# A two-layer attention and expert kernel: no background turn in the 16-key unit, two more pairs summed by VectorE at chunk ends, and a rearranged end

## The chip, the cores and the metric

The kernel runs on one core of a Trainium2 chip (trn2). The metric is the device time of one execution, in microseconds, as the median of several runs. A difference of 0.2% (12 us) is about what can be told from no change here.

## The reference, cut to what matters

```python
# x: (8, 128, 36, 36); 8 images, 128 channels, 1296 positions each
x = x + layer0(group_norm(x))      # 3x3 convolutions to q, k, v; softmax attention
                                   # (1296 queries, 34*34 keys); 1x1 convolutions, tanh
t = tokens(x)                      # (8, 1296, 128)

# layer 1, attention: additive scores
q, k = ln(t) @ Wq.T + bq, ln(t) @ Wk.T + bk
s = einsum('bijd,d->bij', tanh(q[:, :, None] + k[:, None]), w) + bw
t = t + einsum('bij,bjd->bid', softmax(s), ln(t))

# layer 1, experts: each of 64 experts chooses 8 tokens of each image
y = ln(t)
probs = softmax(y @ gate_w.T + gate_b, axis=tokens)      # per image and expert
topv, topi = top_k(probs over tokens, 8)
pooled = sum over the 8 of topv * y[topi]                # (64, 8 images, 128)
h = gelu(pooled @ weight1 + bias1); o = h @ weight2 + bias2
out = t + scatter_add(o * topv at topi)
```

## The kernel before

**The scores.** The sum over 128 channels of w·tanh(q+k) is written as 24 fractions, 16 over groups of 5 channels and 8 over groups of 6. For each fraction the numerator and the denominator are products of exponential features of the keys (`kf`) and of the queries (`qf`) over 32 or 64 rows. A **unit** is one tile of keys against one **chunk** of 432 queries: 8 images x 3 chunks x 11 key tiles. Ten key tiles have 128 keys and take 12 **slots** `k` = 0 to 11, each a pair of fractions; the eleventh has the 16 keys that remain and takes 2 slots. This **16-key unit** stands sixth in the list `order`, so a chunk has positions 0 to 4 (full units), 5 (the 16-key unit) and 6 to 10 (full units). Position 10 is the chunk's end. In all there are 2928 slots.

**A slot.** TensorE makes the denominators of the slot three ahead (`d`, L1086 and L1091, PSUM pool `ps_d` of 2 buffers) and the numerators of this slot (`n`, the same lines, one bank each of the 4-bank pool `ps_n`). ScalarE takes the logarithm (`lq`, L1109) and exp(-log) (L1112). VectorE multiplies numerator and reciprocal. For slots in `DVE_PAIRS` = (1, 4, 7, 10) VectorE multiplies in place in PSUM (L1137) and also adds the products to `accd` (L1139). For the others it writes the products to `rp` (L1143), and GpSimd adds these to `accp` (L1150, L1152). At a unit's end GpSimd folds `accp` and `accd` together (L1159, L1161), except in the very last unit, where VectorE does that; ScalarE takes the exponential of the score (`e`, L1172) seven slots later.

**The background.** The rest of the work is written as generators that yield between steps, in four lanes: `first_of_all` (the eight query feature blocks `pq` of the next chunk; scores of the 16-key unit), `urgent` (`attend`, the weighted sum of values, and keys), `gates` (expert gating of the image before), and `background` (layer 0 and the tokens and keys of the next image). A lane step that needs TensorE runs only in a **turn**, `matmul_turn` after slots 2, 5, 8 and 11, and after slot 1 of the 16-key unit. In the slot after the 16-key unit there is a turn for `first_of_all` alone. Each slot adds `PACE` ns to a balance, each step subtracts what `behind` says it costs, and no lane but `first_of_all` gets a step while the balance is below zero. PSUM tiles of lane steps (`aux`) come from the same 4 banks as the numerators. An engine carries out its instructions in the order written, so what stands behind a waiting instruction waits too.

Of the steps, one matters below. In layer 0's attention GpSimd adds up the exponentials of a chunk's 10 key tiles (`total`, L476, tile `tot`); a matmul with ones sums `tot` over partitions (`pt`), ScalarE inverts it (`ri`, L499 and L500).

**The end.** After the last slot the pools of the scores are closed, and ten weight tiles of 1 MB (`wts`) take their place in SBUF. Both are stacked from the same side. SyncE's queue then holds, in this order: ten weight loads (`load_next`, L1343 and L1345); the last chunk of `t2d`; the gates of images 0 to 6 from DRAM (21 loads, L1361); residual 4 (L1366); the store of image 7's gates (L987); residuals 5 to 7 (L1383); image 7's gates; the other 21 weight loads, each when a buffer comes free; the output. Meanwhile image 7's last chunk goes through `attend`, `gate_logits` and `gate_tokens` (softmax over tokens, `max` for the eight largest, `match_replace` to take them out, the difference, transposes, `ppool`), and then 16 groups of 4 experts run (`inner`, `turned`, `outer`).

Of the kernel before, what the change touches and what calls it, by code (L numbers as in the profile page):

```python
# [10 lines left out]
AF = mybir.ActivationFunctionType  # L11
# [44 lines left out]
LAG = 3  # L56
SHIFT = 6.5
DVE_PAIRS = (1, 4, 7, 10)
TURNS = (2, 5, 8, 11)
NEXT_AT = {k: IN_TURN[i : i + 2] for k, i in zip(TURNS, (1, 3, 5, 7))}  # L60
PACE = 400

# [9 lines left out]
def kernel(  # L72
# [56 lines left out]
    with ExitStack() as loop, ExitStack() as score:  # L129
# [9 lines left out]
        one = pool("one", 1, ctx)  # L139
        chunks = pool("chunks", 8)  # L140
        two = pool("two", 2)
        kfp = pool("kfp", 3, score, "right")
        kstp = pool("kstp", 3, score, "right")
        qfp = pool("qfp", NF + 1, score, "right")
        lp = pool("lp", 2, score, "right")
        rpp = pool("rpp", 3, score, "right")
        acc = pool("acc", 2, score, "right")
        ps_d = pool("ps_d", 2, score, "right", bass.MemoryType.PSUM)

        ps_n = pool("ps_n", 4, space=bass.MemoryType.PSUM)  # L150
# [120 lines left out]
        def matmuls(rest=0):  # L271
            return (True, rest)
# [338 lines left out]
        def tokens(b):  # L611
# [8 lines left out]
            for g in range(0, NKT, 4):  # L620
                tp = aux("tpl")
                some = list(range(g, min(g + 4, NKT)))
                for t in some:
                    o, n = KT[t]
                    turned_to(
                        tp[:n, (t - g) * C : (t - g + 1) * C], r[:, o : o + n], ident
                    )
                yield TAKE
                full = sum(KT[t][1] == 128 for t in some)
                nc.vector.tensor_copy(  # L630
                    tok[:, g : g + full, :],
                    tp[:, : full * C].rearrange("p (t c) -> p t c", c=C),
                )
# [38 lines left out]
            for g in range(0, NKT, 4):  # L672
                tp = aux("tpc")
                some = list(range(g, min(g + 4, NKT)))
                for t in some:
                    o, n = KT[t]
                    turned_to(
                        tp[:, (t - g) * 128 : (t - g) * 128 + n], xh[:n, t, :C], ident[:n, :n]
                    )
                yield TAKE  # L680
                lo, hi = KT[g][0], KT[some[-1]][0] + KT[some[-1]][1]
                nc.vector.tensor_copy(xT[:, lo:hi], tp[:, : hi - lo])
                yield matmuls()
# [204 lines left out]
        def gate_logits(b, chunks):  # L888
# [2 lines left out]
            t2, mv = attended[b]  # L891
            if b not in logits:
                logits[b] = (
                    big_tile("probs")[:E, :N],
                    small.tile([E, NCH], F32, tag="mx", name="mx"),
                )
            pr, mx = logits[b]
# [6 lines left out]
            def turned(c, name):  # L904
# [2 lines left out]
                    turned_to(tp[:, j * T : (j + 1) * T], t2[:T, c * TPC + j, :], ident[:T, :T])  # L907
                return tp, chunk_tile(name)

            for c in chunks:  # L910
                tp, tt = turned(c, "t2T")
                yield TAKE
                nc.vector.tensor_copy(tt, tp[:, :CH])
                nc.sync.dma_start(t2d[b][:, c * CH : (c + 1) * CH], tt)
                yield matmuls(1)
                for j0 in range(0, TPC, 2):
                    tp = aux("tp3")
                    for j in (j0, j0 + 1):
                        turned_to(tp[:T, j * C : (j + 1) * C], tt[:, j * T : (j + 1) * T], ident)
                    yield TAKE  # L920
                    behind[0] += 500
                    for j in (j0, j0 + 1):
                        t = c * TPC + j
                        nc.vector.tensor_scalar(
                            t2[:T, t, :], tp[:T, j * C : (j + 1) * C],
                            mv[:, t, 0:1], rs[:, t - tiles[0] : t - tiles[0] + 1],
                            ALU.subtract, ALU.mult,
                        )
                    yield matmuls()
            for c in chunks:  # L930
# [8 lines left out]
                    pr[:, c * CH : (c + 1) * CH], pg[:E, :CH], gb_s, None, ALU.add, ALU.max,  # L939
                    accum_out=mx[:, c : c + 1],  # L940
                )
                yield matmuls()

        def gate_tokens(b):


            t2, _ = attended.pop(b)
            pr, mx = logits.pop(b)
# [5 lines left out]
            inv = small.tile([E, 1], F32, tag="ginv", name="ginv")  # L954
            tot = small.tile([E, NCH], F32, tag="tot", name="tot")
            gt = big_tile("gt")[:E, :N]
            if b == NB - 1:
                nc.scalar.activation(pr, pr, AF.Exp, bias=nm, accum_out=tot[:, 0:1])
                nc.vector.reciprocal(inv, tot[:, 0:1])
                nc.scalar.activation(pr, pr, AF.Copy, scale=inv)  # L960
                nc.vector.max(out=top, in_=pr)
                nc.vector.match_replace(out=gt, in_to_replace=top, in_values=pr, imm_value=0.0)
                nc.vector.tensor_sub(gt, pr, gt)
            else:
                parts = [slice(c * CH, (c + 1) * CH) for c in range(NCH)]
                tops = gt[:, : NCH * 8].rearrange("p (c k) -> p c k", k=8)
# [17 lines left out]
                for cols in parts:  # L984
                    yield step()
                    nc.gpsimd.tensor_sub(gt[:, cols], pr[:, cols], gt[:, cols])
            nc.sync.dma_start(gd[b], gt)  # L987
            yield matmuls(3)
            half = NT // 2
            gT = []  # L990
            for g in range(2):
                tp = aux("tpg")
                for j in range(half):
                    t = g * half + j
                    turned_to(
                        tp[:T, j * E : (j + 1) * E], gt[:, t * T : (t + 1) * T], ident[:E, :E]
                    )
                yield TAKE
                gT.append(chunk_tile("gT")[:T, : half * E].rearrange("p (t e) -> p t e", e=E))
                nc.vector.tensor_copy(  # L1000
                    gT[g], tp[:T, : half * E].rearrange("p (t e) -> p t e", e=E)
                )
                yield matmuls(g)
            pp = aux("ppool")
            for t in range(NT):
# [270 lines left out]
        for p, (u, k) in enumerate(slots):  # L1276
# [61 lines left out]
        def load_next():  # L1338
# [199 lines left out]
```

## Time and profile before

| | before |
|---|---|
| median of 3 runs (lowest to highest) | 6026.3 us (6025.81 to 6030.31) |
| the profiled execution, and its span | 6030.93 us, 6028.9 us |
| TensorE busy / VectorE / ScalarE / GpSimd | 94% / 79% / 89% / 76% |
| mean granted TensorE clock | 0.991 |
| first and last logarithm (L1109) | 135.7 and 5883.6 us |
| last three weight loads asked for, from | 5987.9 us |

The span runs from the first to the last instruction of the profiled execution. Nearly all of it is the slot loop, from 136 to 5884 us. About 136 us precede it, and about 145 us follow. Busy shares are means over stages that have different limits, so the loop is read by units: the logarithm of each slot (L1109) occurs once per slot, and its start times cut the trace into units. "Unit (b, c, p)" below is image b, chunk c, position p, from the logarithm of its slot 3 to that of the next unit's slot 3.

### The profile page before, as it was taken

Reading aid. Unit: us, or ns where it says so; the run is one execution under the profiler, and the core shown is the slowest. Engines: PE = TensorE matmul, PEld = TensorE weight load, DVE = VectorE, ACT = ScalarE, POOL = GpSimd, SP = SyncE. Lnnn points to the kernel's source line nnn. Section 1 sums busy time; section 2 is a strip of 40 time slices with the busy share of each in tenths; the row PEclk is TensorE's granted clock in tenths of the full one; section 3 lists DMA queues with packets and bytes.
Section 4 is the critical chain, followed back from the end, with each engine's and each line's share of the span. In section 5 each row is a group of like instructions: output and inputs, shape, how many; then the busy total and the mean of one; then the engine's idle time right before and its main releaser. Section 6 shows DMA issues by size and latency. Waiting matters only on the chain.

```text
span 6028.9 us, 94410 instructions
## 1 busy us (share of the span) xinstructions
PE 5641.8 (94%) x33489; PEld 2944.7 (49%) x33489; DVE 4783.2 (79%) x9560; ACT 5358.1 (89%) x5993; POOL 4581.8 (76%) x2870
## 2 busy tenths in 40 slices
PE   8999999999999999999999999999999999988887
PEld 5554455545554454544545445554445544544433
DVE  4887878878887788877888777887878878788883
ACT  2999998999989999889998999999998998999991
POOL 5777877877778868878787777777877777787871
PEclk9999999999999999999999999999999999999997
DMA  1200021001110011100111001110011001110008
GB/s 60 70 23 23 29 72 40 24 22 45 58 42 21 23 61 42 42 23 22 65 38 39 23 25 61 42 36 23 25 63 52 21 25 34 66 50 26 28 21 291
DMA packets 150457, 270.43 MB, mean 45 GB/s; under 512 B 45600, under 2 KB 75680, under 8 KB 149984
## 3 DMA queue, kind: packets, MB, share of 16 engines
q1 hardware_dynamic: 149984, 264.39, 13.3%
q8 instruction: 264, 4.33, 0.3%
q14 instruction: 209, 1.71, 0.1%
HBM read 200.15 MB, written 63.93 MB: 44 GB/s over the span
## 4 chain that ended last, share of the span: by engine, by line
PE 58%; DVE 23%; ACT 8%; issue 7%; POOL 2%; DMA 1%; DVEq 0%; POOLq 0%; ACTq 0%
PE d L1086 19%; PE n L1086 12%; DVE rp L1143 9%; PE pa L278 7%; DVE n L1137 7%; ACT lq L1109 6%; PE pc L278 5%; DVE accd L1139 4%; PE s L278 3%; PE pk L278 3%; PE pq L278 2%; PE n L1091 1%; POOL accp L1152 1%; PE d L1091 1%; DMA w<-in_weight_dram 1%
## 5 line engine op out<-in xcount | busy, mean ns | idle before, releaser
L1152 POOL TENSOR_TENSOR accp<-accp,rp 128x864 f32<-128x864 f32 x1439 | 2911.1, 2023 | 965.9 <-DVE rp L1143 937.9
L1086 PE MATMUL n<-qf,kf 32*128 32x432 f32 (+1 forms) x11520 | 2996.1, 552 | 12.5 <-ACT qf L805 7.4
L1086 PE MATMUL d<-qf,kf 32*128 32x432 f32 (+1 forms) x11520 | 2777.8, 558 | 206.0 <-ACT lq L1109 196.8
L1109 ACT ACTIVATE lq<-d 128x864 f32<-128x864 f32 x2928 | 2480.2, 876 | 341.5 <-PE n L1086 254.3
L1143 DVE TENSOR_TENSOR rp<-n,lq 128x432 f32<-128x432 f32 x3912 | 2182.0, 600 | 701.6 <-PE n L1086 570.6
L1112 ACT ACTIVATE lq<-lq 128x864 f32<-128x864 f32 (+1 forms) x1944 | 2495.9, 1284 | 61.6
L1086 PEld LDWEIGHTS d<-qf,kf 32*128 32x128 f32 (+1 forms) x11520 | 1029.1, 184 | 1359.2 <-ACT lq L1109 992.2
L1086 PEld LDWEIGHTS n<-qf,kf 32*128 32x128 f32 (+1 forms) x11520 | 1260.1, 185 | 668.1 <-issue 287.8
L1139 DVE TENSOR_TENSOR accd<-n,accd 128x432 f32<-128x432 f32 x1440 | 867.9, 603 | 24.7
L1137 DVE TENSOR_TENSOR n<-n,lq 128x432 f32<-128x432 f32 x1440 | 809.8, 608 | 48.5 <-PE n L1086 28.3
L1150 POOL TENSOR_TENSOR accp<-rp 128x864 f32<-128x864 f32 x240 | 485.2, 2021 | 250.3 <-DVE rp L1143 249.7
L278 PE MATMUL pa<-xh,e 128*108 128x129 f32 x1920 | 252.5, 281 | 34.5 <-DVE accd L1139 29.8
L278 PEld LDWEIGHTS pa<-xh,e 128*108 128x108 f32 x1920 | 221.4, 174 | 123.0 <-DVE accd L1139 97.6
L1161 POOL TENSOR_TENSOR accd<-accp,accd 128x432 f32<-128x432 f32 x239 | 265.1, 1109 | 18.7
L1159 POOL TENSOR_TENSOR accp<-accp 128x432 f32<-128x432 f32 x239 | 263.7, 1103 | 12.2
L806 POOL TENSOR_SCALAR qf<-qf,cs_s 128x432 f32<-128x432 f32 x192 | 260.1, 1364 | 4.1 <-ACT qf L805 4.0
L476 POOL TENSOR_TENSOR tot<-tot,e 116x432 f32<-116x432 f32 x192 | 211.8, 1103 | 18.1 <-ACT e L485 14.7
L278 PE MATMUL s<-q,k 128*116 128x432 f32 x480 | 209.6, 547 | 9.7 <-DVE accd L1139 7.6
L278 PE MATMUL pa<-e,vw 116*128 116x432 f32 x480 | 203.0, 546 | 0.0
L485 ACT ACTIVATE e<-s 116x432 f32<-116x432 f32 x240 | 118.8, 521 | 85.7 <-PE s L278 83.1
L278 PEld LDWEIGHTS pk<-xT,a_k 128*128 128x128 f32 x1408 | 165.6, 193 | 57.9 <-DVE accd L1139 42.9
L278 PE MATMUL pk<-xT,a_k 128*128 128x128 f32 (+1 forms) x1408 | 180.7, 281 | 2.4 <-DVE accd L1139 1.4
(246 smaller groups left out, 3764.8 us busy)
## 6 DMA issues: line engine op xcount, KB each, us to landing
kf<-kd SPq DMA_DIRECT2D x239, 512.0 KB
kd<-ks SPq DMA_DIRECT2D x158, 256.0 KB
w<-in_weight_dram SPq DMA_DIRECT2D x32, 1024.0 KB
wk_t<-wk_t_d SPq DMA_DIRECT2D x7, 768.0 KB
wv_t<-wv_t_d SPq DMA_DIRECT2D x7, 768.0 KB
wq_t<-wq_t_d SPq DMA_DIRECT2D x7, 768.0 KB
x<-in_x_dram SPq DMA_DIRECT2D x8, 648.0 KB
t<-tokd SPq DMA_DIRECT2D x96, 54.0 KB
```

What stands on the lines that cost most here:

```text
L278: mm(out, lhsT, rhs, **kw)
L806: nc.gpsimd.tensor_scalar(qf[:, 1, :], qf[:, 0, :], feat["cs_s"][:, q : q + 1], None, ALU.mult)
L1086: mm(outs[h][:, :CH], kf[rows[h], q, :], qf_of[b, c, q][rows[h], part, :], start=True, stop=True)
L1109: nc.scalar.activation(lq[:, o : o + n, :], d[:, :n, :CH], AF.Ln)
L1112: nc.scalar.activation(some, some, AF.Exp, scale=-1.0)
L1137: mult(ns[h], ns[h], lq[:, o + h, :])
L1139: nc.vector.tensor_add(live["d"], ns[h], live["d"])
L1143: mult(rp[:, h, :], n, lq[:, o + h, :])
L1150: nc.gpsimd.tensor_add(live["p"], live["r"], rp)
L1152: ending(u if k == NP - 1 else 0).tensor_add(live["p"], live["p"], rp)
L1159: ending(u).tensor_add(s[:, 0, :], s[:, 0, :], s[:, 1, :])
L1161: ending(u).tensor_add(d, s[:, 0, :], d)
```

## The change

1. The 16-key unit has no turn any more. The turn for `first_of_all` in the slot after it stays.
2. `PACE` is 430 instead of 400, and the copies in `tokens` count 400 ns each in `behind`.
3. In the last unit of each chunk, slots 3 and 9 are treated as the pairs of `DVE_PAIRS`: VectorE adds the products, and GpSimd has two additions fewer.
4. The score pools are created in the reverse order.
5. At the end: filler matmuls (`keep_awake`) before the last `attend` and in `gate_tokens` of image 7; for the last chunk the normalisation is applied to `t2` in place instead of to a twice-transposed copy; for image 7 the eight largest are taken per chunk among the logits, then among the 24 of these; the exponentials of all and of the rest are taken apart, their difference is left unscaled, and the scale is multiplied in after the transposes. Residual 4 is loaded with residuals 5 to 7.

```diff
+MORE_PAIRS = (3, 9)
-PACE = 400
+PACE = 430
...
+        acc = pool("acc", 2, score, "right")
+        rpp = pool("rpp", 3, score, "right")
+        lp = pool("lp", 2, score, "right")
+        qfp = pool("qfp", NF + 1, score, "right")
         kfp = pool("kfp", 3, score, "right")
         kstp = pool("kstp", 3, score, "right")
-        qfp = pool("qfp", NF + 1, score, "right")
-        lp = pool("lp", 2, score, "right")
-        rpp = pool("rpp", 3, score, "right")
-        acc = pool("acc", 2, score, "right")
...
                 yield TAKE
+                behind[0] += 400
                 full = sum(KT[t][1] == 128 for t in some)
...
                 yield TAKE
+                behind[0] += 400
                 lo, hi = KT[g][0], KT[some[-1]][0] + KT[some[-1]][1]
...
+            at_end = b == NB - 1 and chunks[-1] == NCH - 1
...
+                if at_end:
+                    for t in tiles:
+                        nc.vector.tensor_scalar(
+                            t2[:T, t, :], t2[:T, t, :], mv[:, t, 0:1],
+                            rs[:, t - tiles[0] : t - tiles[0] + 1], ALU.subtract, ALU.mult,
+                        )
...
-                for j0 in range(0, TPC, 2):
+                for j0 in () if at_end else range(0, TPC, 2):
...
+                if b == NB - 1:
+                    nc.vector.max(
+                        out=pr[:, N + 8 * c : N + 8 * c + 8], in_=pr[:, c * CH : (c + 1) * CH]
+                    )
...
+        def keep_awake(n):
+
+            ps = aux("idle")
+            for i in range(n):
+                mm(ps, ones, feat["a_k"][:, :512], start=True, stop=True)
...
             if b == NB - 1:
-                nc.scalar.activation(pr, pr, AF.Exp, bias=nm, accum_out=tot[:, 0:1])
+                keep_awake(6)
+                nc.vector.max(out=top, in_=scores[:, N : N + 8 * NCH])
+                nc.vector.match_replace(out=gt, in_to_replace=top, in_values=pr, imm_value=-1e30)
+                all_of = big_tile("all")[:E, :N]
+                nc.scalar.activation(all_of, pr, AF.Exp, bias=nm, accum_out=tot[:, 0:1])
                 nc.vector.reciprocal(inv, tot[:, 0:1])
-                nc.scalar.activation(pr, pr, AF.Copy, scale=inv)
-                nc.vector.max(out=top, in_=pr)
-                nc.vector.match_replace(out=gt, in_to_replace=top, in_values=pr, imm_value=0.0)
-                nc.vector.tensor_sub(gt, pr, gt)
+                nc.vector.tensor_scalar(each, ident[:E, :E], inv, None, ALU.mult)
+                for g in range(2):
+                    cols = slice(g * N // 2, (g + 1) * N // 2)
+                    nc.scalar.activation(gt[:, cols], gt[:, cols], AF.Exp, bias=nm)
+                    nc.vector.tensor_sub(gt[:, cols], all_of[:, cols], gt[:, cols])
+                nc.scalar.activation(all_of, gt, AF.Copy, scale=inv)
...
-            nc.sync.dma_start(gd[b], gt)
+            nc.sync.dma_start(gd[b], all_of if b == NB - 1 else gt)
...
+            if b == NB - 1:
+                ps = aux("each")
+                mm(ps[:T, :E], ones[:E, :T], each, start=True, stop=True)
+                shares = chunk_tile("shares")[:T, :E].rearrange("p (x e) -> p x e", x=1)
+                nc.vector.tensor_copy(shares[:, 0, :], ps[:T, :E])
...
+                if b == NB - 1:
+                    nc.vector.tensor_mul(gT[g], turned_gt, shares.to_broadcast([T, half, E]))
+                else:
+                    nc.vector.tensor_copy(gT[g], turned_gt)
...
+        def ends_chunk(u):
+            return units[u][2] == order[-1]
...
-            if k in DVE_PAIRS and not rem:
+            if not rem and (k in DVE_PAIRS or k in MORE_PAIRS and ends_chunk(u)):
...
-                p, k == 1 if rem else k in TURNS or behind_rem,
+                p, not rem and (k in TURNS or behind_rem),
...
+        keep_awake(4)
         urgent.run(len(slots))
...
-        res.append(big_tile("res")[:, :N])
-        nc.sync.dma_start(res[4], t2d[4])
         drain(gate_tokens(NB - 1))
```

More of the change, by code (lines that the diff above doesn't have):

```diff
@@ L893, in gate_logits @@
                 logits[b] = (
-                    big_tile("probs")[:E, :N],
+                    big_tile("probs")[:E],
                     small.tile([E, NCH], F32, tag="mx", name="mx"),
@@ L941, in gate_logits @@
                 )
+                if b == NB - 1:
+                    nc.vector.max(
+                        out=pr[:, N + 8 * c : N + 8 * c + 8], in_=pr[:, c * CH : (c + 1) * CH]
+                    )
                 yield matmuls()
+        def keep_awake(n):
+            ps = aux("idle")
+            for i in range(n):
+                mm(ps, ones, feat["a_k"][:, :512], start=True, stop=True)
         def gate_tokens(b):
             t2, _ = attended.pop(b)
-            pr, mx = logits.pop(b)
+            scores, mx = logits.pop(b)
+            pr = scores[:, :N]
             nm = small.tile([E, 1], F32, tag="nm", name="nm")
@@ L954, in gate_tokens @@
             inv = small.tile([E, 1], F32, tag="ginv", name="ginv")
+            if b == NB - 1:
+                each = chunk_tile("each")[:E, :E]
             tot = small.tile([E, NCH], F32, tag="tot", name="tot")
@@ L999, in gate_tokens @@
                 gT.append(chunk_tile("gT")[:T, : half * E].rearrange("p (t e) -> p t e", e=E))
-                nc.vector.tensor_copy(
-                    gT[g], tp[:T, : half * E].rearrange("p (t e) -> p t e", e=E)
-                )
+                turned_gt = tp[:T, : half * E].rearrange("p (t e) -> p t e", e=E)
+                if b == NB - 1:
+                    nc.vector.tensor_mul(gT[g], turned_gt, shares.to_broadcast([T, half, E]))
+                else:
+                    nc.vector.tensor_copy(gT[g], turned_gt)
                 yield matmuls(g)
```

## The prediction

> **What bounds the kernel now.** I read the page first, then a table by stretches cut at unit boundaries, then the chain of waits by engine, then the timeline around the costliest wait, and SyncE's own waits for the end.
>
> From the page:
>
> ```profile
> PE 5641.8 (94%) x33489; PEld 2944.7 (49%) x33489; DVE 4783.2 (79%) x9560; ACT 5358.1 (89%) x5993; POOL 4581.8 (76%) x2870
> ...
> L1152 POOL TENSOR_TENSOR accp<-accp,rp 128x864 f32<-128x864 f32 x1439 | 2911.1, 2023 | 965.9 <-DVE rp L1143 937.9
> ...
> L1139 DVE TENSOR_TENSOR accd<-n,accd 128x432 f32<-128x432 f32 x1440 | 867.9, 603 | 24.7
> ```
>
> A GpSimd addition of one pair takes 2.02 us; the two VectorE additions that replace it take 0.60 us each. No engine is full on average, so stretches decide. The table by stretches has, in each row, the stretch, its length, then busy time and instruction count of PE, PEld, DVE, ACT and POOL, the clock, the DMA share and GB/s. In order: a unit with no background (7,1,3); a 16-key unit with a turn (3,0,5), one without (3,2,5), one of image 7 (7,0,5); a chunk end (3,2,10); the first units of chunks 1 and 2 (3,1,0), (3,2,0), and (1,2,0).
>
> ```profile
> 5517.99:5538.41 20.42, 15.43 (x96) 6.11 (x96) 17.34 (x32) 20.17 (x22) 16.38 (x10) 1.00 0.06 18
> 2434.69:2441.38 6.69, 6.69 (x52) 3.29 (x54) 3.28 (x9) 3.43 (x4) 6.03 (x7) 1.00 0.40 121
> 2927.91:2932.90 4.99, 4.99 (x63) 1.69 (x61) 2.96 (x7) 3.33 (x4) 3.43 (x3) 1.00 0.17 31
> 5336.46:5340.39 3.93, 3.93 (x55) 1.40 (x47) 2.50 (x7) 3.32 (x5) 3.77 (x4) 1.00 0.32 99
> 3025.65:3049.64 23.99, 23.66 (x110) 9.94 (x110) 17.13 (x32) 23.74 (x29) 23.75 (x16) 1.00 0.07 22
> 2559.97:2584.69 24.72, 23.55 (x159) 14.40 (x159) 20.62 (x44) 20.49 (x23) 20.05 (x13) 1.00 0.13 39
> 2810.45:2839.70 29.25, 25.07 (x136) 13.37 (x140) 20.46 (x41) 23.03 (x28) 21.34 (x14) 0.94 0.08 26
> 1358.82:1386.64 27.82, 23.66 (x136) 12.88 (x140) 20.38 (x41) 23.03 (x28) 21.39 (x14) 1.00 0.09 28
> ```
>
> Three readings. A quiet unit is ScalarE's (20.17 of 20.42 us). A chunk end is full on ScalarE (23.74 of 23.99) and on GpSimd too (23.75), since eight `qf` scalings of 1.36 us (L806) come on top. The first unit of chunk 2 is 4.5 us longer than that of chunk 1, with fewer matmuls (136 against 159). TensorE's waits name the cause:
>
> ```profile
> PE pt L278 <- POOL tot L476: 20.5, 12, 3.1
> ```
>
> In the timeline GpSimd works without a pause from 2783.9 to 2818.5 us; `tot` stands near the back of that list and ends at 2816.3, and `pt`, with all of TensorE behind it, waits 3.11 us until then. This recurs in images 1 to 6.
>
> For the end, the stretches 5892 to 5919, to 5949 and to 6002, and a line of SyncE's waits:
>
> ```profile
> 5892.00:5919.00 27.00, 14.30 (x61) 10.98 (x61) 13.98 (x36) 3.94 (x6) 0.52 (x2) 0.56 0.98 363
> 5919.00:5949.00 30.00, 28.94 (x226) 12.11 (x225) 5.25 (x13) 5.46 (x8) 2.01 (x7) 0.76 0.83 230
> 5949.00:6002.00 53.00, 40.20 (x423) 20.40 (x423) 9.91 (x27) 5.37 (x9) 2.01 (x7) 0.87 1.05 386
> ...
> SPq L1343 <- DVE accd L1161: 65.4, 1, 65.4
> ```
>
> The end is set by the weight stream: 386 GB/s in the long stretch, begun at 5891.98 when VectorE's last sum was done, with a slack middle in which SyncE issues 21 small gate loads at 0.64 us each.
>
> **What the Trainium skill says.** "GPSIMD Engine Reference", section 3.1, has GpSimd 1.96 times as slow as VectorE on a two-input addition; the trace has 2.02 against 1.06 us for one 864-wide addition (L1152 on VectorE in the last unit), which agrees. "TensorE: Matmul & The Clock Gate", Part 1, says that an idle window of about 3.4 us halves TensorE's clock; the trace agrees in kind: after the `pt` wait the clock is 0.94 over (3,2,0), matmuls of 0.53 us take 0.92, and that unit is 1.4 us longer than (1,2,0), where the clock stayed at 1.00. "DMA: Bandwidth & Descriptors", Specifications, gives 435 GB/s as the fabric's ceiling; the stream has 386, so there is little above it.
>
> **The change, part by part.** I stepped the pacing rule over the same list of lane steps, with slot numbers, to see where work comes to stand.
>
> *The `pt` wait.* With the new pace and no turn in the 16-key unit, the last `tot` of images 1 to 6 moves from slot 11 of (b,1,10) to slot 8, and `pt` from slot 2 of (b,2,0) to slot 11 of (b,1,10). GpSimd's list up to that `tot`, from the folding of the unit before: folding 2.2, slot 2's addition 2.0, slots 5, 6 and 8 6.1, six `qf` 8.2, `tot` 1.1: 19.6 us from 2788.3 of image 3 (where that folding starts now), so 2807.9, or 2808.8 if the last two `qf` come late from ScalarE. TensorE would reach `pt` at about 2808.6 (that turn begins at 2807.7 with one `pq`). So the wait goes from 3.1 to some 0.4 us. Without the two additions moved to VectorE the list would have one more of 2.0 us before `tot`, and a wait of about 2 would stay. Gain: 29.25 - 24.7 = 4.5 us in four images with the lowered clock (2, 3, 4, 6; their units are 29.2 to 29.5), 27.8 - 24.7 = 3.1 in two (1 and 5): 24, less 6 x 0.4: **-22 us**. Bounds 0 and -26.
>
> *The 16-key unit.* Fourteen of them have a turn (chunks 0 and 1 of images 0 to 6). They take 6.7 us, against 5.0 without a turn in chunk 2 and 3.9 to 4.1 in image 7: 1.7 to 2.7 removed. The work itself stays: 12 convolution matmuls in chunk 0, or 6 of 432 columns in chunk 1, are done in other turns. There 42 convolution matmuls lengthen unit (3,0,8) from 20.4 to 23.4, 0.07 each, and 20 of the wide ones lengthen (3,1,8) from 20.4 to 24.2, 0.19 each: 0.8 and 1.1 us back. Net 0.9 and 0.6 by the lower value, which I take as that unit also has work just ahead: 7 x 1.5 = **-10 us**. Bounds: 0 (a stretch of 14 slots around the unit is no longer with the turn, work counted, than one without) and -24.
>
> *More sums by VectorE.* 24 chunk ends x 2 pairs x 2 additions of 0.60 us: 2.4 us more for VectorE in a unit where it is busy 17.1 of 24.0. Queued behind these on VectorE are the multiplications of slots 4 and 10, and the banks of slots 3, 4, 9 and 10 come free up to 1.2 us later. The `pq` of turns 5 and 11 wait for them, the next denominators stand behind those, and ScalarE waits for the denominators. In (3,2,10) `pq` of turn 5 would start about 1.05 us later, and denominators that now end 0.6 us before ScalarE takes them would come 0.4 late; at turn 11 they end 1.2 us ahead, and nothing shows. 24 x 0.4 = **+10 us**. Bounds: 0, and both turns in full, 24 x 2 x 1.05 = +50. GpSimd's own 4.0 us per chunk end I credit with nothing beyond `pt`; its other releases cost VectorE 0.2 us a unit.
>
> *Pace and token costs.* The same steps at nearly the same places: the last step of the next image's keys is in (b,2,8) either way. Nothing, hidden by linear cost per matmul; bounds -5 and +5.
>
> *The end.* The ten weight tiles fill 80 of the 89 KB that the score pools leave, stacked from the same side; that the first load waited for `accd` shows that the first tile lies over the pool created last. After the change `kfp` is there, last read by the last numerators, which end at 5887.0. Slot 9's bank, held 1.2 us longer, delays these to about 5888. The stream starts 4 us earlier, and SyncE's order behind it is the same but for residual 4. **-4 us**; bounds 0 and -6. The shorter work from logits to `ppool` (one scale and one difference of 1.4 to 1.5 us less in sequence, four transposes less, per-chunk `max` of some 0.5 us more) and the filler (12 instructions in `gate_tokens` of 0.43 to 0.86 us, 5 to 10 us, in what was an idle time of 8.7) I cost at nothing: the eleventh weight load waits for SyncE until 5943, over 15 us after `inner` of group 1 has freed a buffer. Were that cover gone, they would be worth -5 to +2.
>
> Sum: -22 - 10 + 10 + 0 - 4 = -26. The profiled execution (6030.9, span 6028.9) would give 6005; it stands 4.6 above the median, to which I apply the sum: **6000 us**.
>
> **Rivals.**
> *VectorE's banks decide (slower).* If the later banks are exposed at turns 5 and 11 of every chunk end, the price is 50 instead of 10 and the time 6040. It decides from 0.75 us per turn (36 us). For it: ScalarE is full there, so every delay shows. Against it: VectorE idles 6.9 us of that unit. 0.11.
> *The wait moves.* If `tot` still comes 3 us after TensorE reaches `pt`, or another step lands on a late GpSimd, only the 16-key unit, VectorE and the end are left: -4, 6022. For it: GpSimd stays near full up to slot 8. 0.15.
> *More of everything.* The 16-key unit gives its 2.7, VectorE's additions hide: -24 - 24 - 5 = -53, 5973. 0.16.
> *The sum as above*, 0.58, its own range 5985 to 6012.
>
> Faster by over 0.2% (12 us, about what a measurement can tell): the sum and the third, 0.74; within: mostly the second, 0.15; slower: 0.11. The range 5970 to 6026 leaves out the first rival and the far end.
>
> **What would show it.** Right: no wait of `pt` for `tot` near 3 us, (b,2,0) near 25 us; 16-key units of 4 to 5 us; chunk ends of 24.0 to 24.8; first weight load about 4 us before the last `accd`. Wrong: chunk ends of 26, or a new wait of TensorE on GpSimd in (b,1,10).

## The result: 6043.9 us, slower, and the profile after

The changed kernel takes 6043.93 us (median of seven runs, 6040.06 to 6055.62), beside 6026.3 for the kernel before: **slower by 17.6 us, ratio 1.003 with a 95% interval of 1.0021 to 1.004**. The forecast was 6000 (5970 to 6026). The profiled execution took 6054.99 us, span 6053.3; the kernel before's was 6030.93. Of the seven runs the three of 6051 us and more, the profiled one among them, have a mean granted clock of 0.991 to 0.992, and the four of 6040 to 6044 one of 0.994 or 0.995, so the profile holds some us that the median does not. Of the 24 us between the two profiles, the slot loop (first to last logarithm) has +24.7 (5747.8 to 5772.5 us), the stretch after it -2.7 (145.4 to 142.7), the start +2.3.

The lines of the page that answer to those of before:

```profile
PE 5632.1 (93%) x33507; PEld 2935.7 (48%) x33507; DVE 4829.2 (80%) x9662; ACT 5360.8 (89%) x5995; POOL 4489.2 (74%) x2822
...
L1191 POOL TENSOR_TENSOR accp<-accp,rp 128x864 f32<-128x864 f32 x1391 | 2815.8, 2024 | 1072.4 <-DVE rp L1182 1051.8
...
L1178 DVE TENSOR_TENSOR accd<-n,accd 128x432 f32<-128x432 f32 x1536 | 924.0, 602 | 26.3
```

The additions moved as the diff says (48 fewer on GpSimd, 96 more on VectorE, at the same durations), and no engine's share rose by more than a point. The 18 us are in no busy total; they have to be read by place.

The table by stretches of the changed kernel, with the same units as before: 16-key units (3,0,5), (3,2,5) and (7,0,5); chunk end (3,2,10); first units (3,1,0), (3,2,0), (1,2,0). Columns as before: the stretch, its length, busy time and count of PE, PEld, DVE, ACT and POOL, clock, DMA share, GB/s.

```profile
2451.21:2456.20 4.99, 4.99 (x63) 1.69 (x60) 2.81 (x8) 3.34 (x4) 4.81 (x5) 1.00 0.24 75
2946.86:2951.84 4.98, 4.98 (x63) 1.68 (x60) 2.91 (x6) 3.33 (x3) 3.72 (x3) 1.00 0.18 55
5365.09:5369.01 3.92, 3.92 (x55) 1.40 (x47) 2.49 (x7) 3.31 (x4) 3.76 (x4) 1.00 0.30 100
3044.26:3068.72 24.46, 23.14 (x110) 10.23 (x110) 18.71 (x35) 23.89 (x29) 20.86 (x15) 1.00 0.07 20
2578.55:2602.55 24.00, 22.64 (x156) 14.09 (x153) 20.54 (x45) 20.61 (x21) 16.52 (x11) 1.00 0.07 23
2833.84:2860.44 26.60, 23.62 (x145) 12.86 (x142) 20.69 (x44) 21.95 (x24) 16.33 (x10) 0.94 0.07 20
1374.97:1401.58 26.61, 23.63 (x145) 13.65 (x142) 20.69 (x44) 21.95 (x25) 16.36 (x10) 0.94 0.06 20
```

The 16-key unit fell from 6.69 to 4.99 us in chunks 0 and 1, as forecast. The first unit of chunk 2 fell from 29.25 to 26.60 here. The clock still reads 0.94 in four of the six images, and there the unit is 26.6; in the two with 1.00 it is 25.0. The light chunk end (3,2,10) went from 23.99 to 24.46.

What had not been shown before are the two chunk ends that hold layer 0's work beside `pq`, (3,0,10) and (3,1,10). First before, then after:

```profile
2535.61:2559.97 24.36, 23.98 (x131) 12.25 (x128) 18.81 (x35) 23.91 (x29) 24.12 (x16) 1.00 0.06 16
2785.15:2810.45 25.30, 24.80 (x120) 10.81 (x117) 18.08 (x34) 24.27 (x30) 25.06 (x18) 1.00 0.07 18
```

```profile
2552.34:2578.55 26.21, 24.98 (x136) 12.37 (x135) 20.67 (x38) 24.24 (x29) 22.36 (x15) 1.00 0.09 29
2806.79:2833.84 27.05, 25.00 (x119) 10.74 (x115) 19.76 (x37) 24.95 (x30) 24.82 (x18) 1.00 0.09 28
```

They are 24.36 and 25.30 us before, 26.21 and 27.05 after: the "chunk ends of 26" that the prediction named as the sign that it was wrong. The sign has more than one cause: in the changed kernel without the two pairs (t_noB below) they are 25.26 and 27.03. TensorE's and SyncE's waits after, two lines each:

```profile
PE pq L279 <- DVE accd L1178: 21.8, 75, 0.6
PE pt L279 <- POOL tot L477: 7.9, 8, 1.2
```

```profile
SPq L1382 <- PE n L1122: 61.7, 1, 61.7
...
SPq L1382 <- ACT e L1211: 4.9, 1, 4.9
```

`pt` waits 7.9 us in all and 1.2 at most, where it waited 20.5 and 3.1: the stall is gone. `pq` waits 21.8 us for `accd` of VectorE, in place of 3.8. The first weight load is released by the last numerators, as forecast; the second then waits 4.9 us for the last exponential.

### The profile page after: what moved, and what is told of

Read it like the earlier page. It is cut to its first block, busy times and chain, and to the rows that moved or that the text cites. A ratio compares the mean times of both kernels' runs of the same rounds, so it can differ in the third digit from the quotient of the medians.

```text
span 6053.3 us, 94409 instructions
## 1 busy us (share of the span) xinstructions
PE 5632.1 (93%) x33507; PEld 2935.7 (48%) x33507; DVE 4829.2 (80%) x9662; ACT 5360.8 (89%) x5995; POOL 4489.2 (74%) x2822
## 4 chain that ended last, share of the span: by engine, by line
PE 49%; DVE 22%; ACT 16%; issue 10%; POOL 1%; DMA 1%; DVEq 0%; ACTq 0%; POOLq 0%
PE d L1122 16%; ACT lq L1145 11%; PE n L1122 10%; DVE rp L1182 8%; DVE n L1176 7%; PE pa L279 7%; PE pc L279 5%; DVE accd L1178 4%; PE s L279 3%; PE pq L279 2%; ACT lq L1148 2%; ACT ks L785 1%; ACT e L1211 1%; PE n L1127 1%; PE d L1127 1%
## 5 line engine op out<-in xcount | busy, mean ns | idle before, releaser
L1191 POOL TENSOR_TENSOR accp<-accp,rp 128x864 f32<-128x864 f32 x1391 | 2815.8, 2024 | 1072.4 <-DVE rp L1182 1051.8
L1182 DVE TENSOR_TENSOR rp<-n,lq 128x432 f32<-128x432 f32 x3816 | 2126.7, 599 | 634.3 <-PE n L1122 494.3
L1178 DVE TENSOR_TENSOR accd<-n,accd 128x432 f32<-128x432 f32 x1536 | 924.0, 602 | 26.3
L1176 DVE TENSOR_TENSOR n<-n,lq 128x432 f32<-128x432 f32 x1536 | 862.5, 607 | 96.7 <-PE n L1122 43.7
L279 PE MATMUL pq<-xT,a_q 128*128 128x432 f32 x384 | 171.5, 559 | 22.0 <-DVE accd L1178 21.8
```

Of the source, the lines that this page charges most:

```text
L279: mm(out, lhsT, rhs, **kw)
L1176: mult(ns[h], ns[h], lq[:, o + h, :])
L1178: nc.vector.tensor_add(live["d"], ns[h], live["d"])
L1182: mult(rp[:, h, :], n, lq[:, o + h, :])
L1191: ending(u if k == NP - 1 else 0).tensor_add(live["p"], live["p"], rp)
```

## The experiments

Every run is of the whole kernel, compared with the kernel before on the same chip. "us" beside a ratio is (ratio - 1) x 6029; an interval of 0.001 either way is 6 us, so a difference of two runs is known to 7 to 9 us. Sums by position are finer, but each is of one execution. Positions and slots are those of the text above. All figures by position are sums over all 24 chunks, profile against profile.

### The parts one at a time

```diff
# t_A: the kernel before, no turn in the 16-key unit
-                p, k == 1 if rem else k in TURNS or behind_rem,
+                p, not rem and (k in TURNS or behind_rem),
# t_B: the kernel before, MORE_PAIRS = (3, 9) at all chunk ends
-            if k in DVE_PAIRS and not rem:
+            if not rem and (k in DVE_PAIRS or k in MORE_PAIRS and ends_chunk(u)):
# t_C: the kernel before, pace and token costs
-PACE = 400
+PACE = 430
+                behind[0] += 400        # twice, in the copies of tokens
# t_D: the changed kernel with these three undone: the end and the order of pools alone
```

> The kernel before, with one edit: no turn in the 16-key unit. Theory 'work returns' (from the trace of the changed kernel): the fourteen 16-key units fall from 6.7 to 5.0 us (-23 in all), and the moved work comes back at positions 6 to 9 at its full price, so the time is 6026 +- 8. Rival 'free turn' (the prediction's step): -10, 6016. A third, that the moved work brings new waits of TensorE: +10 or more, with pt waiting for tot at another place.

> The kernel before, with one edit: slots 3 and 9 of a chunk's last unit added by VectorE. Theory 'banks': in chunk ends with background work (chunks 0 and 1 of images 0 to 6) the later banks hold up pq and what follows, +1.8 us each, +25 in all; the wait of pt for tot in the first unit of chunk 2 shrinks by up to 2 of 3.1 us, -12 to -20; sum +5 to +13, 6031 to 6039. Rival 'hidden' (the additions cost nothing, the 1.8 us at chunk ends came from where the turns' work now stands): the pt gain alone, 6006 to 6014, with chunk ends at 24.4 and 25.3 us as before.

> The kernel before, with one edit: pace 430 instead of 400 and 400 ns more for each of the copies of tokens. The prediction's step: no change, 6021 to 6031. Rival 'crowding': more steps fall into one turn, so ScalarE starves in turns with 6 or 8 wide matmuls while other turns stay empty: +10 to +20, 6036 to 6046.

> The kernel before, with the changed end alone (order of the score pools, fillers, in-place normalisation, eight largest among logits, residual 4 later); the loop's turns, pace and VectorE's slots as before. The prediction's step: -4, the stretch behind the last logarithm 141 us instead of 145, 6022. Rival: the order of the pools or the fillers cost time elsewhere: 6026 or more.

Measured: t_A 0.9977 (0.9969 to 0.9985), -14 us; t_B 0.9998 (0.999 to 1.0006), -1; t_C 1.0011 (1.0003 to 1.002), +7; t_D 0.9995 (0.9987 to 1.0003), -3. They add up to -11, and the whole is +18. The profiles say why. In t_A, t_B and t_C alike the `pt` wait is gone: 3.0, 7.7 and 2.8 us in all are left of 20.5. Each part removes the same stall by itself, so three single runs have its gain in them and the whole change has it once. If the stall is worth some 20 us, the parts without it cost about +5, +18 and +26. Only t_D came out as expected: t_A has the size of its rival, but from the stall, t_B is below its 5 to 13, and t_C lies between its two cases.

### The stall by itself

Two ways to remove it. t_S only moves `pt` (and the rest of that lane) two slots later, to slot 5 of (b,2,0). t_Bskip leaves out part of the computation: at chunk ends the products of slots 3 and 9 are made and then added by nobody, so GpSimd's list is shorter by the two additions and VectorE's no longer.

```diff
# t_S
-                        yield matmuls(3)
+                        yield matmuls(3 if c < NCH - 1 else 5)
# t_Bskip
+                elif k in (3, 9) and units[u][2] == order[-1]:
+                    pass
                 elif k == 0:
                     live["r"] = rp
```

> The kernel before, with one edit: the last pt of each layer 0 rests two slots longer, so that it falls in slot 5 of the first unit of chunk 2 instead of slot 2. Theory 'one stall counted three times' (the edits tried alone, without the turn, with the two pairs, with the pace, each shortened that unit from 29 to 24 or 25 us): the wait of pt for tot goes, -18 to -24, 6006 to 6013 beside a before of 6030, with nothing else changed. Rival: the shorter unit is paid for later in the chunk: -5 or less.

> Before, but in the last unit of each chunk the products of slots 3 and 9 are made as before and then added by nobody: part of the sum is left out. GpSimd has the two additions fewer that the change takes from it, and VectorE has no addition more. Theory, VectorE's additions cost 18 us at the chunk ends: the stall at chunk 2's first unit goes (-12) and chunk ends stay at 24.0 to 25.3 us, so about 6017 (ratio 0.998; 0.997 to 0.999). Rival, the chunk ends grow because GpSimd's earlier release lets other work come sooner, and not by VectorE's time: as with the additions on VectorE, 6029 (1.0), chunk ends of 25.8 and 26.3.

Measured: t_S 0.9982 (0.9975 to 0.999), -11; t_Bskip 0.9969 (0.9958 to 0.9981), -19, where 12 had been expected. Units (3,0,10), (3,1,10), (3,2,0) of t_Bskip:

```profile
2530.14:2554.50 24.36, 23.98 (x131) 12.26 (x128) 18.80 (x35) 23.92 (x29) 21.03 (x15) 1.00 0.06 16
2780.02:2805.34 25.32, 24.82 (x120) 10.82 (x117) 18.07 (x34) 24.30 (x31) 23.75 (x17) 1.00 0.07 14
2805.34:2830.74 25.40, 23.90 (x136) 12.87 (x140) 20.35 (x41) 23.04 (x28) 18.72 (x13) 1.00 0.11 36
```

The chunk ends are as before (24.36, 25.32), the first unit of chunk 2 has gone from 29.25 to 25.40, and its clock from 0.94 to 1.00. By position, position 0 has -22.5 us and no other more than 1.5. **The stall is worth about what the prediction's first step said: 22 by position, 19 in the time.** In t_S the same wait vanishes and (3,2,0) falls to 24.6, but the steps that `pt` holds up move along, and positions 1 and 2 pay 12 us.

### VectorE's additions, with the stall gone in both

t_B is t_Bskip with the additions on VectorE: 0.9998 against 0.9969, so they cost **18 us**. The same two chunk ends of t_B:

```profile
2537.19:2562.99 25.80, 24.29 (x133) 12.41 (x132) 20.82 (x39) 24.07 (x28) 21.03 (x15) 1.00 0.07 21
2788.06:2814.35 26.29, 25.11 (x120) 11.57 (x117) 19.81 (x37) 24.29 (x30) 23.18 (x17) 1.00 0.06 18
```

25.80 and 26.29 us; VectorE is busy 20.82 and 19.81, and TensorE's wait for its banks has grown (t_B, then t_Bskip):

```profile
PE pq L279 <- DVE accd L1143: 27.3, 81, 0.6
```

```profile
PE pq L278 <- DVE accd L1139: 3.7, 20, 0.2
```

Cut into the intervals between logarithms (mean of images 1 to 6; the interval named by its turn ends with the first logarithm that the turn can delay), the price sits in three places:

```
chunk end of      behind turn 5       behind turn 11      unit
                  t_Bskip   t_B       t_Bskip   t_B       t_Bskip   t_B
chunk 0            3.77     4.31       3.01     3.91       24.36    25.80
chunk 1            4.35     5.33       2.97     2.97       25.31    26.30
chunk 2            3.47     3.58       2.97     2.97       24.00    24.11
```

The prediction read its 0.4 off (3,2,10), where the measured price is 0.11. The end of chunk 0 has `pvw` matmuls of layer 0 beside `pq` in turns 5 and 11, and that of chunk 1 has four `pa` in turn 5. 3.47 and 2.97 are the intervals of a turn with `pq` alone. So the reading is: where other work already makes the interval longer, if only by 0.04 us, the slack has been spent, and a pair costs 0.5 to 1.0.

Two runs test that in one unit, with the same additions on VectorE and the same one fewer for GpSimd: a pair at the ends of chunk 1 alone, slot 9 (t_E9) or slot 3 (t_E3).

```diff
-            if k in DVE_PAIRS and not rem:
+            if not rem and (k in DVE_PAIRS or k in (9,) and units[u][1:] == (1, order[-1])):
# t_E3: (3,) in place of (9,)
```

> Before, with VectorE adding the products of slot 9 in the last unit of chunk 1 alone (8 units). GpSimd's list ahead of tot is 2.0 us shorter, so the stall at chunk 2's first unit falls from 3.1 to about 1.1 us and the clock stays up: 3.4 us less in four images, 2.0 in two, -18. Theory, a pair costs what the slack of its own turn doesn't cover: slot 9's stands before turn 11, where in chunk 1 nothing showed, so (b,1,10) stays at 25.3 us and the whole gives about 6011 (ratio 0.997; 0.996 to 0.998). Rival, each pair costs its share of the 18 us measured for 48 pairs, 0.4 us: +3, 6014 (and the interval behind turn 11 of chunk 1 longer by 0.4).

> The same with slot 3 in place of slot 9 (last unit of chunk 1 alone). The stall falls alike, -18. Theory of the turn's own slack: slot 3's pair stands before turn 5, which in chunk 1 has other work beside pq, and costs 0.98 us in each of 8 units: +8, so about 6019 (ratio 0.9983; 0.997 to 0.9995), with (b,1,10) at 26.3. Rival, the price is VectorE's time wherever it lies: as t_E9.

Measured: t_E9 0.997 (0.9959 to 0.9982), -18; t_E3 0.9985 (0.9978 to 0.9991), -9. Unit (3,1,10) of t_E9, then of t_E3:

```profile
2780.00:2805.30 25.30, 24.73 (x120) 11.28 (x117) 18.81 (x35) 24.27 (x31) 25.07 (x18) 1.00 0.06 17
```

```profile
2778.93:2805.23 26.30, 25.21 (x120) 11.10 (x117) 19.10 (x36) 24.29 (x31) 25.07 (x18) 1.00 0.06 17
```

VectorE and GpSimd do the same number of additions; 25.30 us against 26.30. Behind turn 5 the interval is 4.35 with slot 9's pair and 5.33 with slot 3's. In this unit it isn't VectorE's time that is paid for, it is the lateness of one turn. What the turn itself holds does not say everything: at the end of chunk 0 of the changed kernel turn 5 has `pq` alone, behind a turn with convolutions, and there slot 3's pair costs 0.68 us (3.47 in t_noB, 4.15 in the whole).

t_Bp was meant to tell the late banks apart from VectorE's time: the pairs of slots 3 and 9 go through `rp` in SBUF as before, and VectorE adds from there, so their own banks come free early.

```diff
+            if not rem and k in MORE_PAIRS and ends_chunk(u):
+                rp = rpp.tile([128, 2, CH], F32, tag="rp", name="rp")
+                for h, n in enumerate(ns):
+                    mult(rp[:, h, :], n, lq[:, o + h, :])
+                for h in range(2):
+                    nc.vector.tensor_add(live["d"], rp[:, h, :], live["d"])
```

> The kernel before with slots 3 and 9 of a chunk's last unit summed by VectorE, but the products go to rp in SBUF first and are added from there: VectorE's work is the same as with the two pairs alone, while the PSUM banks come free as early as before. Theory 'banks': chunk ends go back to 24.4 and 25.3 us (25.8 and 26.3 with the pairs alone), and the time falls to 6010 to 6016. Rival 'VectorE's time': chunk ends stay at 25.5 and 26, 6025 to 6032.

Measured: 1.0036 (1.0023 to 1.0049), +22, 23 us more than t_B. Its row for the new additions (count, then least, median and longest in ns) says that the comparison isn't clean:

```profile
L1138 DVE TENSOR_TENSOR accd<-rp,accd x96: 596/616/1682, 368.8 to 5907.1; 128x432 f32<-128x432 f32 x96
```

The additions from SBUF take 840 ns in the mean and up to 1682, where those from PSUM take 585 to 609. So this way of releasing the banks of slots 3 and 9 early is no remedy, since `pq`, behind the same VectorE queue, waited longer than ever (55.5 us for `accd`). How much of the 23 us is the slower addition the run doesn't say, and so it doesn't decide between late banks and VectorE's time; t_E9 and t_E3 rule out the latter, for their unit.

### Pace

t_C gives +7 without a stall. A turn is called heavy here when its matmuls make 1500 columns of output or more (one of layer 0's makes 432). By the stepped rule there are 33 heavy turns in the kernel before, 73 at pace 430, 82 in the whole change, and fewer turns used in all (799, 785, 769). Counted in the traces the heavy ones are 18, 58 and 67: other totals, the same steps. Two runs change that number: t_Ccap has pace 430 with a limit on a turn, t_C460 a pace of 460.

```diff
# t_Ccap: t_C, and
+            begun = behind[0]
             while turn:
-                    paced = balance[0] < 0
+                    paced = balance[0] < 0 or behind[0] - begun >= 1000
# t_C460: t_C with PACE = 460
```

> Before with the new pace and token costs, and one line more: a turn begins no further step (but for first_of_all) once its steps have counted 1000 ns or more. Stepping the rule gives turns of 1500 columns or more: 33 before, 73 with the pace and token costs, 42 with this limit too (791 turns in place of 785), while the last pt of images 1 to 6 stays at (b,1,10), slot 2. Theory, crowding (long turns cost more than the same work in shorter ones): the pace's own cost of about 18.5 us beyond the stall is for some 40 heavy turns, 0.46 each; 9 are left, so +4 and -12 for the stall, about 6021 (ratio 0.9986; 0.9975 to 0.9995). Rival, the pace costs because work comes earlier in the chunk, beside other work, whatever its parcels: as with the pace alone, 6036 (1.001).

> Before with pace 460 and the token costs, a larger step of the same kind: by the stepped rule 129 turns of 1500 columns or more (33 before, 73 at pace 430), 733 turns used in place of 799. Theory, crowding: 96 x 0.46 = +44, less 12 for the stall: about 6061 (ratio 1.0053; 1.003 to 1.008). Rival, the cost lies in where the work falls at 430 and not in the size of turns: about as at 430, 6036 (1.001), or less, as the background is done earlier and the last units of the image have none.

Measured: t_Ccap 0.9985 (0.9978 to 0.9991), -9; t_C460 1.0106 (1.0091 to 1.0122), +64. Taken from t_Bskip's -19, where the stall is gone and the pace old: 42 heavy turns cost +10, 73 cost +26, 129 cost +83. The limit brings 16 of the 26 us back with the pace left at 430, which speaks against the rival (where the work lies, whatever its parcels); but a limit moves work too, so size and place aren't quite parted. The price isn't one figure for each heavy turn either: with the stall at 19 us instead of 12 it is 1.1 us with the limit, 0.65 at 430 and 0.86 at 460. Pace and token costs came together in t_C; from t_C to t_C460 only the pace changes. A lower granted clock is not the cause in the whole change: the run at its median has 0.994, as that of t_noC (below) has.

TensorE's wait for ScalarE in t_Bskip, t_C and t_C460 shows the other side:

```profile
PE d L1086 <- ACT lq L1109: 201.4, 393, 2.0
```

```profile
PE d L1088 <- ACT lq L1111: 246.7, 456, 2.0
```

```profile
PE d L1088 <- ACT lq L1111: 307.9, 530, 2.0
```

Work that is packed into fewer turns leaves others empty. There TensorE can't run ahead, since the denominators have two buffers, and waits for the logarithm: 45 and 106 us more in all, and 39 and 96 of these stand in the slots behind an empty turn (135 us there in t_Bskip, 174 in t_C, 232 in t_C460). Mean length of the three slots behind a turn, by the matmul instructions that the turn held (nine of the traces, sorted, so an observation and not an experiment), with the count of such turns. `pk` makes the features of the keys; `s`, `pa` and `pt` are the scores, the weighted sums and the sum over partitions of layer 0's attention; `pc` and `px` are its convolutions. A matmul of the program shows as two instructions:

```
turn holds        mean us    before   t_C   t_C460
nothing             5.23       171    186     243
8 pk                5.08         7      1       0
16 pk               6.06        67     58      44
24 pk               6.83         9     16      18
4 pa                5.49         7      7       9
4 s                 5.87        27     22      10
4 pa + 2 s          6.28        62     48      46
4 pa + 4 s          6.87         1     21      21
12 pc               6.24        89     71      74
12 pc + 2 px        7.13         0     14       0
4 pa + 2 pt + 2 px  7.72         0      0      20
```

The first small parcel is nearly free (8 `pk`: nothing; 4 `pa`: 0.26 us), the next is not (8 more `pk`: 0.98). 8 `pk` and 16 `pk` in two turns take 11.14 us, 24 `pk` and an empty turn 12.06.

### Parts left out of the whole, and versions to keep

```diff
# t_noB: the changed kernel
-MORE_PAIRS = (3, 9)
+MORE_PAIRS = ()
# t_noC: the changed kernel with PACE = 400 and without the 400s of tokens
```

> The kernel after, without the two pairs at chunk ends. If the pairs cost what the kernel with them alone shows once the stall's gain is counted once (chunk ends +18 us, some +5 elsewhere): 6044 - 20 = 6024, unless the wait of pt, now in slot 11 of the chunk's last unit, grows from 1.2 to 3 us without GpSimd's relief: then 6035.

> The kernel after, with pace 400 and without the 400 ns of the token copies. Theory 'crowding' (turns with more than about 7 wide matmul instructions rise from 25 to 74 with pace 430 by stepping the rule, at 0.5 us each): -25 to -30, 6015 to 6019. Rival: the pace is harmless once the stall is gone: 6040 to 6048.

Measured: t_noB 1.0014 (1.0007 to 1.0021), +8; t_noC 0.9997 (0.9989 to 1.0005), -2. Beside the whole change's +18, VectorE's additions are worth +10 there and the pace +20. Both runs missed what was expected: 20 us for the additions, or a wait of `pt` of 3 us without them, where it is 1.4 at most; and 25 to 30 us for the pace. The additions cost less in this company because, at the end of chunk 1, `pt` and four `pa` lie in turn 11 now and set its interval (5.99 us without the additions, 6.01 with them).

Three versions put together what was worth something: t_AD has no turn in the 16-key unit and the new end; t_E69D has the new end and slots 6 and 9 to VectorE at the ends of chunk 1; t_E9D has slot 9 alone.

```diff
# t_AD: the changed kernel, MORE_PAIRS = (), old pace and token costs
# t_E69D: t_D with
+MORE_PAIRS = (6, 9)
+            if not rem and (k in DVE_PAIRS or k in MORE_PAIRS and units[u][1:] == (1, order[-1])):
# t_E9D: the same with MORE_PAIRS = (9,)
```

> Before, with two parts of the change: no turn in the 16-key unit, and the changed end with its order of pools. Each part has its own place, so the two should add: about -14 from the first alone (most of it the stall at chunk 2's first unit, which the moved pt avoids) and about -2.5 from the second (the weight stream begun when the last numerators are done). Expected about 6013 us beside a before of 6029, a ratio of 0.9972 (0.996 to 0.998), 16-key units of 5.0 us in image 3, (3,2,0) near 23.6 to 25, chunk ends as before, after the last logarithm about 143. If the gain of the first part was only its luck with one placing of the turns, or the second only moves the start, 6020 or more.

> Before, with the changed end and order of pools, and with VectorE adding the products of slots 6 and 9 in the last unit of chunk 1 alone. GpSimd has 4.0 us less ahead of tot: the stall goes whole, -22.5; the end gives -3. Theory: slot 9's pair is free, and slot 6's stands before turn 8, which has pq alone and an interval as short as that of a turn without work, but no known slack: between 0 and 0.5 us a unit, +2. About 6006 (ratio 0.9961; 0.995 to 0.997). Rival: turn 8 pays in full as turn 5 did, 1 us in each of 8 units, 6012.

> Before, with the changed end and order of pools, and with VectorE adding the products of slot 9 alone, in the last unit of chunk 1 alone. The parts lie in different places and should add: -18 from slot 9's pair, measured by itself, and -3 from the end: about 6008 (ratio 0.9965; 0.9955 to 0.9975), (b,1,10) at 25.3 us, (3,2,0) at 25.7, 142 to 143 us after the last logarithm. If they don't add, 6011 or more.

Measured: t_AD 6013.16 us, 0.9973 (0.9964 to 0.9983), the sum of its parts. t_E69D 6014.66, 0.9975 (0.9965 to 0.9985), a miss for two reasons. The stall didn't go whole: `pt` still waits 11.4 us for `tot` in all, (b,2,0) stays at 26.2 us in images 1 to 6, and position 0 gains 16.4 us and not 22.5; why so much is left isn't shown. And at the chunk end the interval behind turn 8 grew by 0.14 us, and that behind turn 11, free with slot 9 alone, by 0.46 (2.97 to 3.43), as if two pairs near each other used one slack. **t_E9D 6007.38 us, 0.9965 (0.9952 to 0.9979)**, the best seen and faster than both kernels: (b,1,10) stays at 25.3 us, (3,2,0) is 25.7, and 141.8 us follow the last logarithm.

## Why the prediction was wrong, step by step

Four runs lead from the kernel before to the changed one, and their differences are the steps' prices in that order, each to 7 or 8 us:

```
step of the sum             predicted    measured as             us
the pt wait                    -22       t_Bskip                -19
more sums by VectorE           +10       t_B from t_Bskip       +18
16-key unit, and the end       -14       t_noC from t_B          -1
pace and token costs             0       whole from t_noC       +20
sum                            -26                              +18
```

**The `pt` wait: right.** -22.5 by the profile's position 0. Its residue is larger than the 0.4 us forecast: in (3,1,10) of the changed kernel `pt` waits 1.15 us.

**More sums by VectorE: right mechanism, term mis-sized.** The turn, the bank and the waiting `pq` were those of the text. The price was worked out at a chunk end of chunk 2, as 0.4, and multiplied by 24. That one pays 0.11; those of chunks 0 and 1 pay 1.44 and 0.99 (t_B). "At turn 11 nothing shows" is right for chunks 1 and 2 and wrong for chunk 0 (0.90).

**The 16-key unit: half of the step failed.** Position 5 gave -22.9 us where 14 x 1.7 = 24 was read. The failing term is "0.8 and 1.1 us back". Its counts were misread ((3,0,8) holds 36 convolution instructions and not 42, (3,1,8) 18 of them and 12 of 432 columns and not 20), but that makes it only 1.0 and 1.1, and the step -9. In t_A everything but position 5 and the stall's 22.5 adds up to +32 us, 2.3 per turn removed and not 0.95. The step's own bound of 0 was the value: t_noC is 1 us from t_B with an end worth 3. Part of the 32 can be seen in unit (b,2,2), which took 21.0 us before. A pause of TensorE of 1.90 us stands there now, and behind it the clock fell in images 2 to 6 and not in image 1; images 1 and 3 of t_A:

```profile
1405.92:1428.41 22.49, 19.58 (x111) 8.15 (x106) 20.31 (x38) 21.74 (x24) 15.79 (x11) 1.00 0.04 7
2853.78:2878.04 24.26, 21.22 (x107) 8.47 (x104) 20.48 (x37) 21.97 (x24) 15.55 (x11) 0.93 0.04 6
```

The unit costs 16 us more in all than in t_Bskip, some 7 of them the clock's. Heavy turns don't explain the rest: by the trace t_A has 14, fewer than the 18 before. Why the moved work costs so much more than the units used for its price stays open.

**Pace and token costs: the step that failed most.** "Nothing, hidden by linear cost per matmul", bounds 5 either way; measured +20, and +26 with the stall gone otherwise. The cost is not linear in the matmuls, whose number stays: the limit on a turn and the pace of 460 move the time the way the number of heavy turns moves. That the last step of the keys comes at the same place says nothing about the parcels in between; the rule had been stepped, but only places were read from it, not the contents of turns.

**The end: right as far as it can be told.** -4 forecast, -2.7 between the profiles, -3 in t_D (within its interval of no change), and 141.8 us behind the last logarithm in t_E9D against 145.7 in t_E9, which lacks the new end. The first weight load was asked for 8.4 us behind the last logarithm before, and 4.7 after; the last three at 104.3 and 101.0.

**Rivals.** "VectorE's banks decide" came close in its number (6040) and on its side, but by luck: its own mechanism brings 10 to 18 of its 50 us, and most of the loss is the pace's, which no case had. "The wait moves" is excluded by the 7.9 us.

## What to carry to other kernels

Where several parts of a change remove one stall, its gain counts once, and each part's other cost shows only against a version in which the stall is gone already. A pacing constant for interleaved work is a choice of parcels: look at the distribution of what single turns hold, not at when the work is done. Price an added operation at each place where it will stand, the fullest ones first; the slack of a quiet place says nothing of them, and two additions near each other may share it.

## What the runs showed of the hardware

TensorE's clock fell after a much shorter pause than the `pt` stall. In (3,2,0) of the changed kernel TensorE has nothing for 1.90 us, since ScalarE does a step of layer 0 ahead of the logarithm that frees `d`; the stretch of that pause, and the one behind it:

```profile
2844.87:2846.77 1.90, 0.00 (x1) 0.00 (x1) 1.25 (x3) 1.87 (x4) 1.79 (x3) 0.99 0.00 0
2846.77:2850.20 3.43, 3.43 (x9) 1.44 (x10) 1.07 (x3) 3.40 (x5) 1.80 (x1) 0.51 0.02 5
```

The clock reads 0.51 over the next 3.4 us. The same pause of 1.90 us stands in (b,2,0) of images 1 to 6, and the clock fell behind it in four of them (1, 3, 4 and 6: 0.70, 0.50, 0.70 and 0.51 over 3.4 us) and stayed at 1.00 in two. Before the change the pause there was 3.1 us, and four of six again were followed by a low clock. In t_A it stands in (b,2,2), 1.90 us long, and five of six were (0.54 to 0.69). So the length of a single pause didn't decide it here. "TensorE: Matmul & The Clock Gate", Part 1, of the Trainium skill has a free-running window of about 3.4 us, so that it counts where in the window a pause falls; that agrees with equal pauses of which only some cost the clock, but these pauses are shorter than the idle window that the page names. In the changed kernel the units with the low clock take 26.6 us and those with 1.00 take 25.0.

VectorE's additions with both inputs in SBUF (t_Bp) took from 596 to 1682 ns. "SBUF — State Buffer", section "SBUF: two separate sides", says that such an instruction and one of GpSimd that reads SBUF exclude each other for their whole length. The spread agrees; it wasn't tested by taking GpSimd's work away. The same sums from PSUM kept to 609 ns at most.
